# Third pair's first layer beside the first two's, attention vectors as columns, bias reliefs by rows, and a new table of priorities

## The chip, the cores and the metric

One core of a Trainium2 chip runs the whole program in one launch. The metric is the device time of one execution in microseconds. TensorE (PE) does matmuls, with its weight loads shown apart (PEld). VectorE (DVE), ScalarE (ACT) and GpSimd (POOL) do elementwise work. SyncE (SP) issues most of the DMAs, and ScalarE's queue issues a few at the start.

## The reference

64 graphs of 256 nodes with 256 features go through two layers, in float32. All that matters here:

```python
# layer 0
def _gat(h, adj, W, a, out_features):
    Wh = h @ W
    e = leaky_relu(Wh @ a[:256] + swap(Wh @ a[256:]), 0.2)
    att = softmax(where(adj > 0, e, NEG), axis=1)
    return att @ Wh
h = _gat(_gat(x, adj, W1, a1), adj, W2, a2)
h = layernorm(x + h, g_ln1, b_ln1)
x = layernorm(h + relu(h @ w_ff1 + b_ff1) @ w_ff2 + b_ff2, g_ln2, b_ln2)
# layer 1, 8 heads of 32
attn = softmax(q @ k.T / sqrt(32))
out = sum over r in 0..3 of (attn * (adj == r)) @ v_r      # adj is 0 or 1 here
x = layernorm(x + out @ Wo + bo, g1, beta1)
x = layernorm(x + gelu(x @ W1 + b1) @ W2 + b2, g2, beta2)
```

## The kernel before

**Pairs.** The kernel works on pairs of graphs, 32 of them. Each pair is a Python generator, `whole_way` (line 1212), that goes through two GAT layers (`gat_layers`, 637), a feed-forward with ReLU (`feed_forward`, 813), the relational attention (`attention`, 955), and a second feed-forward with GELU. Several pairs are on their way at once. Large products are done by a 2x2 block scheme with seven products in place of eight (`Blocks`, 470; `by_seven`, 887). Every matmul of 128 output columns is issued as four strips of 32 (`by_strips`, 161), each in two instructions.

**The order is planned in Python, when the program is built.** `run` (286) simulates the engines with a clock for each. The generators yield steps of TensorE, each with the events it needs, a number of PSUM banks and the buffers it takes. Pieces for the other engines are queued with `put` (221), with an estimated duration. At each turn the engine that can begin first begins. Among several pairs with a step ready, TensorE takes the one of lowest `degree` (294), and another engine takes the piece of lowest `rank`. At most `flight` pairs are on their way. `CHANGES` (32) alters ranks, degrees, `slack`, `flight` and the order of the block products ("first", "qkv") at given planned times. `START`, `LANDED` and `THERE` (67 to 69) are times the planner assumes for the first loads. The order that comes out is fixed: each engine runs its instructions in it.

**The start.** W1·W2 with the attention vectors beside it is made on the chip as `w12`, 260 columns (168 to 189): DVE multiplies W2's rows with a broadcast a2 and sums them (line 179), TensorE multiplies by W1's transpose, and DVE and ScalarE copy. The two a1 columns are loaded on ScalarE's queue (176). Meanwhile SP issues the loads of all weights, with those of the first three pairs (`EARLY`) between them (1142 to 1165).

**GAT layers.** For each graph pair: the product with `w12` (`ps<-w,...`, 260 columns), copies out of PSUM by ScalarE (642), exponentials of the attention columns (`addends`, 558, into a tile `rise`), then their rows spread over all partitions into a tile `rows`. For the first two pairs (`HURRIED`) this is done by TensorE (587) with ScalarE copies (590). For the others DVE turns the tile (597), and SP stores it to memory (601) and loads it back spread (605). `gat_weights` (612) forms the weights `e` on DVE (lines 622 and 624) and scales the values on ScalarE (631), and TensorE multiplies (`ps<-xw,e` or `ps<-v,e`). The values lie in two buffers `xw`, and those of pair 1 in the attention's buffer `v`. A pair from the third on waits until the pair before has begun its second layer's product and the pair before that is through its GAT layers:

```python
yield [loads[0], *([z_begun[pair - 1], through_gat[pair - 2]] if pair > 1 else [])], None, 2, *(["xw"] * (pair != 1))
```

**Reliefs.** Layer norm's scale and shift are handled so that a stage's output bias is added to the residual in advance. What this adds to the next stage's input must be taken out of that stage's bias: `relieve` (1172) computes bias minus W^T times the added vector, one column of output per matmul (line 1179, 128x128 weights and a moving operand of one column). It runs for the first feed-forward, q and k, and the second feed-forward. After each, DVE forms sums of weight blocks for the block scheme (438, 432).

**The end.** In the last stage `by_seven` leaves sums of rows to ScalarE (`means`, 705, line 712), then squares (726), the root on POOL (731, 732), two DVE passes (737, 740) and the store to `out` (1222), each for two tiles of rows at a time: graph 0, then graph 1.

Of the kernel before, what the change touches and what calls it, by code (L numbers as in the profile page):

```python
# [10 lines left out]
F32 = mybir.dt.float32  # L11
# [19 lines left out]
NORMED = ()  # L31
CHANGES = (
    (27.0, ("rank", "centre", 2),
     ("all", "first", ("a1", "b1", "a2", "a6", "b2", "b6", "a5", "a7", "b7", "b5", "a4", "b4", "a3"))),
    (117.0, ("rank", "piece", 3), ("rank", "halves", -1)),
    (207.0, ("all", "slack", 0.4), ("rank", "exp", -2), ("rank", "scale", 2)),
    (297.0, ("degree", "gat", -1)),
    (387.0, ("degree", "first", -1)),
    (477.0, ("rank", "halves", 2), ("rank", "v", -0.5)),
    (567.0, ("all", "slack", 0.1)),  # L40
    (657.0, ("all", "first", ("a1", "b1", "b2", "a2", "a6", "b6", "a5", "a7", "b7", "b5", "a4", "b4", "a3"))),
    (747.0, ("all", "slack", 0.6), ("rank", "act", -1), ("rank", "turn", 0), ("rank", "divide", 0), ("degree", "fill", 1.5),
     ("rank", "qk", 2)),
    (837.0, ("rank", "mask", -0.5), ("rank", "centre", 2)),
    (927.0, ("rank", "addends", 2)),
    (1017.0, ("rank", "means", -2), ("rank", "sums", -2), ("all", "slack", 0.4)),
    (1197.0, ("rank", "mask", 1)),
    (2187.0, ("rank", "mask", -0.5)),
    (2277.0, ("rank", "exp", -0.5), ("rank", "halves", -0.5)),
    (2457.0, ("rank", "squares", 3)),  # L50
    (2547.0, ("all", "slack", 0.3)),
    (2637.0, ("rank", "normalise", 1.5), ("degree", "first", 2)),
    (2727.0, ("rank", "centre", 1), ("rank", "turn", 1), ("all", "slack", 0)),
    (2817.0, ("all", "slack", 0.2), ("rank", "means", 3)),
# [6 lines left out]
        "normalise": -1, "copies": -2, "seeds": -2, "act": -1, "last": -1, "sums": -0.5, "qk": 1, "v": 1.5, "exp": 3, "mask": 0, "halves": 0, "invert": 3,  # L61
# [5 lines left out]
START = {"tensor": 9.5, "vector": 9.3, "scalar": 9.7, "gpsimd": 0.0, "sync": 36.0}  # L67
LANDED = (("ln0", 15.0), ("ff0", 18.5), ("ff0_last", 26.0), ("ln1", 28.5), ("attention", 34.5), ("ff1", 40.0), ("ff1_last", 43.0))
THERE = ((6.5, 8.0, 13.5), (9.5, 11.0, 27.5), (20.5, 22.0, 35.0))
# [3 lines left out]
def two_layers(ctx: ExitStack, tc: tile.TileContext, t: dict, out: bass.AP, flag: bass.AP):  # L73
# [22 lines left out]
    PART = 64  # L96
# [74 lines left out]
    a2, w1T = passing[:, 0], passing[:, 1].rearrange("p (c m) -> p c m", c=KC)  # L171
    junk = work.tile([P, 2, N], F32, name="h", bufs=HQ)[:, 0]
    nc.sync.dma_start(right[:, :, :D], t["L0_gnn_W2"].rearrange("(c p) m -> p c m", p=P))
    nc.scalar.dma_start(w1T, t["L0_gnn_W1T"].rearrange("(c p) m -> p c m", p=P))
    nc.scalar.dma_start(a2, bass.AP(tensor=t["L0_gnn_a2"].tensor, offset=t["L0_gnn_a2"].offset, ap=[[0, P], [1, 2 * D]]))
    nc.scalar.dma_start(right[:, :, D + 2:], t["L0_gnn_a1c"])
    for s in range(2):
        for c in range(KC):
            nc.vector.scalar_tensor_tensor(
                junk, right[:, c, :D], 1.0, a2[:, s * D:(s + 1) * D], op0=ALU.mult, op1=ALU.mult,  # L180
                accum_out=right[:, c, D + s:D + s + 1])
    both = [bank() for _ in range(KC)]
    for m in range(KC):
        for columns in (slice(0, D), slice(D, D + 4)):
            for c in range(KC):
                by_strips(both[m][:, columns], lhsT=w1T[:, c, m * P:(m + 1) * P], rhs=right[:, c, columns],
                          start=c == 0 and columns.start == 0, stop=c == KC - 1, skip_group_check=True)
    nc.vector.tensor_copy(w12[:, 0], both[0][:, :D + 4])
    nc.scalar.activation(w12[:, 1], both[1][:, :D + 4], AF.Copy)

# [7 lines left out]
               for at, *each in CHANGES for of, name, value in each]  # L202
# [3 lines left out]
                                             ("input", 1), ("rows", 1), ("e", 2), ("adj", 4), ("sums_yT", 1), ("sums_yTa", 1), ("x", 4))}  # L206
# [151 lines left out]
    def done_with(name):  # L358
        del alone[name]

# [197 lines left out]
    def addends(y, there, at, layer, pair):  # L558
# [9 lines left out]
        def largest():  # L568
            nc.vector.tensor_reduce(steep[:, pair, layer:layer + 1], y[:, :, at:at + 2], axis=AX.XY, op=ALU.max,
                                    apply_absolute_value=True)  # L570

        def exps():
            e1 = y[:, :, at].rearrange("p (b j) -> p b j", b=2)
            nc.scalar.activation(of_kind[:, 0::2], e1, AF.Exp, bias=shift[:, 0:1])
            nc.scalar.activation(of_kind[:, 1::2], e1, AF.Exp, bias=shift[:, 0:1], scale=ALPHA)
            nc.scalar.activation(ratio, y[:, :, at + 1], AF.Exp, scale=ALPHA - 1.0)

        put("vector", 0.15, largest, *there, rank=3)
        there = put("scalar", 0.6, exps, *there, rank=rank_of["exps"], function="exp")
        if pair < HURRIED:  # L580
            yield [there], None, 4, "rows"
            at_home["rows"] = rows = work.tile([P, 8, 4, 32], F32, name="rows")
            copied = []
            for n in range(4):
                p = bank()
                for j in range(2):
                    nc.tensor.transpose(p[:, j * P:(j + 1) * P], rise[:, j, 8 * n:8 * n + 1].to_broadcast([P, P]), ident)

                def copy(n=n, p=p):
                    nc.scalar.activation(rows[:, :, n], p[:, :N].rearrange("p (q c) -> p q c", q=8), AF.Copy)  # L590

                copied.append(put("scalar", 0.33, copy, took(0.3), rank=0, frees=["bank"]))
            return at_home, ratio, copied
# [14 lines left out]
        there = put("vector", 0.2, turn, there, rank=rank_of["addends"])  # L608
# [3 lines left out]
    def gat_weights(y, at, at_home, ratio, there, to, b):  # L612
# [3 lines left out]
        def weigh(j):  # L616
            k = 2 * b + j
            if j == 0:
                of["e"] = work.tile([P, 2, N], F32, name="e", bufs=2)
# [13 lines left out]
        there = put("vector", 0.93, lambda: weigh(0), *there, rank=rank_of["weigh"] + b / 2, needs="e")  # L633
        there = put("vector", 1.13, lambda: weigh(1), there, rank=rank_of["weigh"] + b / 2, frees=["rows"] * b)
        return of, put_each("scalar", 0.4, [lambda j=j: scale(j) for j in range(2)], there, rank=rank_of["ratios"])

    def gat_layers(pair, to, loads):
        yield [loads[0], *([z_begun[pair - 1], through_gat[pair - 2]] if pair > 1 else [])], None, 2, *(["xw"] * (pair != 1))
        y = in_values if pair == 1 else work.tile([P, 4, D + 4], F32, name="xw", bufs=2)

        def evacuated(to, k, wide, ps):
            return put("scalar", 0.27, lambda: nc.scalar.activation(to[:, k, :wide], ps[:, :wide], AF.Copy),
                       took(0.88), rank=rank_of["evac"], frees=["bank"])

# [11 lines left out]
        at_home, ratio, there = yield from addends(y, there, D + 2, 0, pair)  # L656
        e = [gat_weights(y, D + 2, at_home, ratio, [loads[1], *there], to, b) for b in range(2)]
        there = []
        for b in range(2):
            yield [e[b][1]], None, 2, *(["xw"] if b == 0 else [])  # L660
            if b == 0:
                happens(z_begun[pair], clock["tensor"])
                z = work.tile([P, 4, D + 4], F32, name="xw", bufs=2)
            for i in range(2):
# [4 lines left out]
                there.append(evacuated(z, 2 * b + i, D + 2, ps))  # L669
            frees_at(clock["tensor"], ["e"])  # L670
        frees_at(clock["tensor"] + 0.2, ["xw"] * (pair != 1))
        at_home, ratio, there = yield from addends(z, there, D, 1, pair)
        e = [gat_weights(z, D, at_home, ratio, there, to, b) for b in range(2)]
        normal = {}
        for b in range(2):
# [7 lines left out]
            frees_at(there.time, ["e"] + ["xw"] * b)  # L683
            added = add_rows(to["x"], ps, b, there, loads[2])
            transposed(to["x"], layernorm(to["x"], ln[0], b, added, biased[0], stage="gat"), normal, b, pair, 0)
# [19 lines left out]
    def means(y, b, *events):  # L705
# [3 lines left out]
        def mean(j):  # L709
            if j == 0:  # L710
                of["less"] = small.tile([P, 2], F32, name="less", bufs=8)
            nc.scalar.activation(unread, y[:, 2 * b + j, :], AF.Copy, scale=-1.0 / D, accum_out=of["less"][:, j:j + 1])
# [3 lines left out]
    def layernorm(r, gb, b, added, *events, stage=None):  # L716
# [3 lines left out]
        rows = [r[:, 2 * b + j, :] for j in range(2)]  # L720
# [7 lines left out]
        def root():  # L728
# [4 lines left out]
            if stage in NORMED:  # L733
                nc.gpsimd.tensor_tensor(of["less"], of["less"], rstd, ALU.mult)
# [7 lines left out]
        def normalise(j):  # L742
            nc.scalar.activation(rows[j], rows[j], AF.Identity, bias=of["less"][:, j:j + 1], scale=rstd[:, j:j + 1])

        def onto_all(n, op):
            both = r[:, of_graph(b), :]
            nc.vector.tensor_tensor(both, both, gb[n].rearrange("p (k d) -> p k d", k=1).to_broadcast([P, 2, D]), op)

        there = put_each("scalar", 0.54, [lambda j=j: square(j) for j in range(2)], there, rank=rank_of["squares"])
        if stage in NORMED:  # L750
            there = put("gpsimd", 1.6, root, there, rank=0)
            there = put_each("scalar", 0.42, [lambda j=j: normalise(j) for j in range(2)], there, rank=rank_of["normalise"])
            return put_each("vector", 0.6, [lambda n=n, op=op: onto_all(n, op) for n, op in ((0, ALU.mult), (1, ALU.add))], there, *events,
                            rank=rank_of["scale"])
# [58 lines left out]
    def feed_forward(y, normal, w, func, relieved, gb, pair, stage):  # L813
# [44 lines left out]
        yield from (by_seven if stage in SEVEN else by_eight)(y, normal, f, evacuated, w2, w2_there, b, order)  # L858
# [829 lines left out]
```

## Time and profile before

| what | us |
|---|---|
| median of 3 runs | 2898.7 (2896.8 to 2900.65) |
| the profiled execution | 2905.58 |
| its span, first to last instruction | 2903.8 |
| TensorE busy in it | 2862.7 |
| mean granted TensorE clock | 0.996 of full |

The profile is one execution. "Busy" for TensorE is from the first to the last of its overlapping matmuls, so that a matmul which runs slowly counts as busy all the same; durations of equal groups must be compared to see this. In rows of the timeline the columns are start, duration, engine, line, operation, tiles, shape and count, with the idle time before it and what ended it in brackets. In rows of the chain they are start, duration, engine and tile. TensorE spends its time as follows (line, engine, operation, tiles, shape and count, then busy time, mean of one in ns, and idle time before):

```profile
L164 PE MATMUL ps<-w_L_gnn_W,ff 128*32 128x128 f32 x14336 | 424.4, 273 | 1.4 <-issue 0.8
L164 PE MATMUL ps<-w_L_gnn_w_ff,ff 128*32 128x128 f32 x14336 | 423.3, 273 | 1.9 <-DVE ff L509 1.1
L164 PE MATMUL ps<-yT,w_L_gnn_W1p 128*32 128x256 f32 x5120 | 307.6, 381 | 4.0 <-DMA yT<-home 2.6
```

These are the feed-forwards' second and first layers, the largest groups; each has a few us of idle time before it in the whole run.

### The profile page before, as it was taken

How to read it: one execution, taken by the hardware profiler on the slowest of the kernel's cores; microseconds unless marked ns; L12 is line 12 of the kernel's file. 1: busy time of each engine (PE TensorE's matmuls, PEld its weight loads, DVE VectorE, ACT ScalarE, POOL GpSimd, SP SyncE). 2: the span in 40 equal slices, each digit the busy share in tenths (PEclk: the TensorE clock that was granted, in tenths of full speed). 3: DMA queues.
4: the chain of work that ended last, by engine and by line, in shares of the span. 5: the costliest groups of instructions: out<-in, count | busy, mean ns of one | idle time of the engine just before them, and what ended most of it. 6: DMA issues, size and time to landing. Idle time of an engine off the chain costs nothing.

```text
span 2903.8 us, 151915 instructions
## 1 busy us (share of the span) xinstructions
PE 2862.7 (99%) x68114; PEld 2021.2 (70%) x68114; DVE 2636.2 (91%) x5873; ACT 1908.4 (66%) x5171; POOL 284.9 (10%) x518
## 2 busy tenths in 40 slices
PE   8999999999999999999999999999999999999997
PEld 5766677676776676676767776766777877767666
DVE  7889998899998999998999999999999999999986
ACT  5656766656766667666677666676666676666765
POOL 0001010101010100001111101101101111010001
PEclk9999999999999999999999999999999999999999
DMA  6222222222222221222222222222222222221100
GB/s 206 75 68 70 69 65 79 72 79 79 65 69 76 83 83 58 78 70 79 79 76 69 69 76 84 74 74 70 72 76 83 76 65 68 83 73 51 54 3 25
DMA packets 207955, 212.11 MB, mean 73 GB/s; under 512 B 22592, under 2 KB 166336, under 8 KB 207040
## 3 DMA queue, kind: packets, MB, share of 16 engines
q1 hardware_dynamic: 206608, 201.79, 21.6%
q8 instruction: 536, 8.78, 1.3%
q14 instruction: 123, 1.01, 0.1%
q10 hardware_dynamic: 688, 0.53, 0.1%
HBM read 137.51 MB, written 64.73 MB: 70 GB/s over the span
## 4 chain that ended last, share of the span: by engine, by line
PE 87%; DVE 6%; DMA 4%; ACT 1%; issue 1%; SPq 1%; ACTq 0%; DVEq 0%; POOL 0%; POOLq 0%
PE ps L164 73%; PE ps L1063 7%; PE ps L1031 4%; PE ps L1066 2%; DMA home<-yb 2%; DVE ff L913 1%; DVE m L1045 1%; DMA yT<-home 1%; SPq L784 1%; DMA rows<-row 1%; DVE x L740 1%; DVE yb L773 1%; DVE h L1049 0%; DVE x L737 0%; DVE x L910 0%
## 5 line engine op out<-in xcount | busy, mean ns | idle before, releaser
L164 PE MATMUL ps<-w_L_gnn_W,ff 128*32 128x128 f32 x14336 | 424.4, 273 | 1.4 <-issue 0.8
L164 PE MATMUL ps<-w_L_gnn_w_ff,ff 128*32 128x128 f32 x14336 | 423.3, 273 | 1.9 <-DVE ff L509 1.1
L164 PEld LDWEIGHTS ps<-w_L_gnn_W,ff 128*32 128x32 f32 x14336 | 393.3, 110 | 41.7 <-issue 19.5
L164 PEld LDWEIGHTS ps<-w_L_gnn_w_ff,ff 128*32 128x32 f32 x14336 | 396.2, 110 | 36.3 <-issue 10.0
L1041 ACT ACTIVATE a<-ps 128x512 f32<-128x512 f32 x512 | 264.3, 601 | 186.5 <-PE ps L1031 180.6
L913 DVE TENSOR_TENSOR ff<-ff 128x1024 f32<-128x1024 f32 x256 | 311.5, 1217 | 55.3 <-PE ps L164 38.9
L731 POOL TENSOR_SCALAR rstd<-squares 128x2 f32<-128x2 f32 x256 | 78.8, 308 | 2591.1 <-ACT unread L726 2590.6
L164 PE MATMUL ps<-yT,w_L_gnn_W1p 128*32 128x256 f32 x5120 | 307.6, 381 | 4.0 <-DMA yT<-home 2.6
L1045 DVE TENSOR_TENSOR m<-a,adj 128x1024 f32<-128x1024 f32 x256 | 307.9, 1215 | 3.7 <-ACT a L1041 3.5
L164 PE MATMUL ps<-yT,w_L_gnn_w_ff1p 128*32 128x256 f32 x5120 | 306.2, 379 | 0.0
L838 ACT ACTIVATE ff<-ps 128x512 f32<-128x512 f32 x384 | 220.9, 587 | 129.6 <-PE ps L164 128.9
L726 ACT ACTIVATE unread<-x,less 128x256 f32<-128x256 f32 x512 | 258.7, 505 | 70.6 <-DVE less L701 54.1
L509 DVE TENSOR_TENSOR ff<-ps,ff 128x512 f32<-128x512 f32 x384 | 255.6, 682 | 38.0 <-PE ps L164 25.2
L1000 ACT ACTIVATE qk<-ps,bqk 128x256 f32<-128x256 f32 x256 | 109.6, 470 | 222.6 <-PE ps L164 222.3
L164 PE MATMUL ps<-xw,e 128*32 128x256 f32 (+1 forms) x4032 | 245.0, 383 | 1.3 <-ACT xw L631 1.3
L164 PEld LDWEIGHTS ps<-yT,w_L_gnn_W1p 128*32 128x32 f32 x5120 | 165.3, 110 | 109.3 <-ACT ff L838 7.5
L164 PEld LDWEIGHTS ps<-yT,w_L_gnn_w_ff1p 128*32 128x32 f32 x5120 | 168.2, 110 | 99.9 <-ACT ff L838 0.5
L737 DVE SCALAR_TENSOR_TENSOR x<-x,less,b_ln 128x256 f32<-128x256 f32 x512 | 227.4, 477 | 7.3 <-ACT unread L726 6.2
L740 DVE SCALAR_TENSOR_TENSOR x<-x,rstd,b_ln 128x256 f32<-128x256 f32 x512 | 229.1, 477 | 1.3 <-POOL rstd L732 1.3
L910 DVE TENSOR_TENSOR x<-ps,x 128x256 f32<-128x256 f32 (+1 forms) x384 | 193.7, 505 | 21.9 <-PE ps L164 17.3
L732 POOL TENSOR_TENSOR rstd<-rstd,mhalf 128x2 f32<-128x2 f32 x256 | 205.5, 803 | 21.3
L164 PEld LDWEIGHTS ps<-xw,e 128*32 128x32 f32 x4032 | 135.7, 111 | 84.1 <-issue 2.6
(141 smaller groups left out, 4992.7 us busy)
## 6 DMA issues: line engine op xcount, KB each, us to landing
home<-yb SPq DMA_DIRECT2D x182, 256.0 KB, 2.2
yT<-home SPq DMA_DIRECT2D x728, 64.0 KB, 2.1
rows<-row SPq DMA_DIRECT2D x60, 512.0 KB, 4.0
x<-in_x SPq DMA_DIRECT2D x32, 512.0 KB, 3.9
out<-x SPq DMA_DIRECT2D x64, 256.0 KB, 2.5
input<-in_xT SPq DMA_DIRECT2D x30, 512.0 KB, 4.1
input<-in_adjT SPq DMA_DIRECT2D x29, 512.0 KB, 4.2
m<-in_adjT SPq DMA_DIRECT2D x3, 512.0 KB, 8.6
```

What stands on the lines that cost most here:

```text
L164: nc.tensor.matmul(to[at:at + DH], lhsT=lhsT[:, at:at + DH], rhs=rhs, **flags)
L509: nc.vector.tensor_tensor(self.target(*where), self.bank["z"], self.target(*where), ALU.add)
L726: nc.scalar.activation(unread, rows[j], AF.Square, bias=of["less"][:, j:j + 1], accum_out=squares[:, j:j + 1])
L732: nc.gpsimd.tensor_tensor(rstd, rstd, mhalf[:, :2], ALU.pow)
L737: nc.vector.scalar_tensor_tensor(rows[j], rows[j], of["less"][:, j:j + 1], g, op0=ALU.add, op1=ALU.mult)
L740: nc.vector.scalar_tensor_tensor(rows[j], rows[j], rstd[:, j:j + 1], beta, op0=ALU.mult, op1=ALU.add)
L838: return put("scalar", 0.5, lambda: nc.scalar.activation(target(c, h), of, AF.Copy), event, rank=rank_of["copies"])
L910: return put("vector", us, lambda: nc.vector.tensor_tensor(to, of, to, ALU.add), *events, rank=rank_of["last"], frees=frees)
L913: return put("vector", 1.14, lambda: nc.vector.tensor_tensor(to, a, b, op), *events, rank=rank_of["sums"])
L1041: nc.scalar.activation(a[n][q][:, k], ps[2 * q + k], AF.Exp)
L1045: nc.vector.tensor_tensor(m[n][q], a[n][q], adj, ALU.mult)
L1063: nc.tensor.matmul(po[o * DH:(o + 1) * DH, :N], lhsT=v[:, b, jc, at:at + DH], rhs=e[o // 2][:, o % 2, jc * N:(jc + 1) * N], start=r == jc ...
```

## The change

Six things are done at once.

1. **Weight setup.** W2's products with a2 are made by TensorE out of W2's transpose and a2's columns, in place of DVE. The four columns of a2 and a1 are one load on SP, second after W2. The wide product no longer waits for them.
2. **The third pair.** Its loads of x transposed and adj are issued right after those of the first two pairs. Its first layer no longer waits for the pairs before. For this, the first two pairs keep the values between their GAT layers in buffers of the attention's exponentials ("a"), with their two attention columns in small tiles of their own (`z_thin`). Pair 1 also has `rows` in a mask buffer ("m") and `e` in buffers of half sums ("h"). `rise` becomes a resource that the planner knows.
3. **Reliefs by rows.** The vector, spread over 32 columns, is the stationary operand, and the weights are the moving one; DVE turns the result into columns.
4. **The last stage of the last pair** is normalised and stored by row halves of both graphs in place of graph by graph.
5. **A new table `CHANGES`**, 25 entries for 20, with `flight` 5 from a planned time of 45.9 to 2673.9, and new assumed times of the first loads.
6. Code that nothing used (`NORMED`) is taken out.

```diff
 CHANGES = (
-    (27.0, ("rank", "centre", 2),
-     ("all", "first", ("a1", "b1", "a2", "a6", "b2", "b6", "a5", "a7", "b7", "b5", "a4", "b4", "a3"))),
-    (117.0, ("rank", "piece", 3), ("rank", "halves", -1)),
...
+    (9.9, ("rank", "rows", 1), ("rank", "exp", -2), ("rank", "ratios", 3), ("degree", "after", 0.5), ("degree", "first", 2.5),
+     ("all", "first", ("a1", "b1", "a6", "a2", "b2", "b6", "a5", "a7", "b7", "b5", "a4", "b4", "a3"))),
...
+    (2673.9, ("rank", "copies", 0), ("all", "flight", 7), ("degree", "attention", -1), ("rank", "qk", 0.5),
+     ("rank", "scale", 3), ("all", "slack", 0.1)),
...
-START = {"tensor": 9.5, "vector": 9.3, "scalar": 9.7, "gpsimd": 0.0, "sync": 36.0}
+START = {"tensor": 9.8, "vector": 9.7, "scalar": 9.7, "gpsimd": 0.0, "sync": 36.5}
...
-    nc.scalar.dma_start(a2, bass.AP(tensor=t["L0_gnn_a2"].tensor, offset=t["L0_gnn_a2"].offset, ap=[[0, P], [1, 2 * D]]))
-    nc.scalar.dma_start(right[:, :, D + 2:], t["L0_gnn_a1c"])
...
+    nc.sync.dma_start(right[:, :, D:], t["L0_gnn_ac"])
+    nc.scalar.dma_start(w2T, t["L0_gnn_W2T"].rearrange("(c p) m -> p c m", p=P))
...
+    wide(0)
+    nc.vector.tensor_copy(w12[:, 0, :D], both[0][:, :D])
+    wide(1)
+    nc.scalar.activation(w12[:, 1, :D], both[1][:, :D], AF.Copy)
+    narrow_columns(thin[0], w2T, slice(D, D + 2))
+    nc.vector.tensor_copy(right[:, :, D:D + 2], thin[0][:, :, :2])
+    narrow_columns(thin[1], w1T, slice(D, D + 4))
+    nc.vector.tensor_copy(w12[:, :, D:], thin[1])
...
-    for pair in range(2):
+    for pair in range(EARLY):
         emit[pair][0]()
         emit[pair][1]()
...
-    emit[2][0]()
-    emit[2][1]()
...
-        yield [loads[0], *([z_begun[pair - 1], through_gat[pair - 2]] if pair > 1 else [])], None, 2, *(["xw"] * (pair != 1))
+        yield [loads[0], *([z_begun[pair - 1], through_gat[pair - 2]] if pair >= EARLY else [])], None, 2, *(["xw"] * (pair != 1))
...
+        def in_parts(z, thin, k, ps):
+            def copy():
+                nc.scalar.activation(z[:, k, :D], ps[:, :D], AF.Copy)
+                nc.scalar.activation(thin[:, k], ps[:, D:D + 2], AF.Copy)
...
-                z = work.tile([P, 4, D + 4], F32, name="xw", bufs=2)
+                z = work.tile([P, 4, D + 4], F32, name="xw", bufs=2) if pair > 1 else rows_in("a")
+                thin = z[:, :, D:D + 2] if pair > 1 else z_thin[pair]
...
-    def relieve(bias, w, rows, more):
+    def relieve(bias, per, w, more):
 
         p = bank()
...
+        for h in range(2):
             for c in range(KC):
...
+                for q in range(HQ):
+                    nc.tensor.matmul(p[q * DH:(q + 1) * DH, h * per * DH:(h + 1) * per * DH],
+                                     lhsT=more[1][:, c:c + 1].to_broadcast([P, DH]),
+                                     rhs=w[:, ((0, 1), (2, 6))[h][c]].rearrange("p (a q j) -> p q a j", q=HQ, j=DH)[:, q],
+                                     start=c == 0, stop=c == KC - 1)
+        turned = p[:, 256:256 + 2 * per * DH]
+
+        def subtract():
+            nc.vector.transpose(turned, p[:, :2 * per * DH])
+            nc.vector.tensor_tensor(bias, bias, turned.rearrange("p (h a i) -> p h a i", h=2, i=DH)[:, :, :, 0], ALU.subtract)
...
-        normal["added"] = [means(y, g, d24, d7, d3) for g in range(2)]
+        if last_of_all(pair, stage):
+            normal["added"] = [means(y, by_halves(j), d24, d7, *([d3] * j)) for j in range(2)]
+        else:
+            normal["added"] = [means(y, pair_of(g), d24, d7, d3) for g in range(2)]
```

## The prediction

> **What bounds the kernel now.** I read the page's busy shares first, then the windows of the middle, then the chain of waits and the timeline of the start, then the end.
>
> ```profile
> PE 2862.7 (99%) x68114; PEld 2021.2 (70%) x68114; DVE 2636.2 (91%) x5873; ACT 1908.4 (66%) x5171; POOL 284.9 (10%) x518
> 1409.00:1497.00 88.00, 88.00 (x2120) 61.63 (x2112) 81.71 (x183) 59.35 (x161) 9.52 (x16) 1.00 0.24 75
> 1481.78 7.08 PE ps L164 x192
> 1569.82 7.08 PE ps L164 x192
> ```
>
> The second line is one window of the middle (length, then busy time of PE, PEld, DVE, ACT, POOL, granted clock, DMA share, GB/s): TensorE is busy in all 88.00 us, VectorE in 81.71. The last two are pieces of the chain of waits: the same piece comes back after 88.04 us, one pair of graphs. 32 pairs at 88.04 are 2817.3 us; the other 86.5 us of the span of 2903.8 are the start, the end and irregular stretches. TensorE's visible idle time is 2903.8 - 2862.7 = 41.1 us. I add the timeline's gaps: 4.56 before its first matmul, 3.8 + 2.1 + 1.3 up to 60 us, and 11.9 after its last matmul (2891.9). So 17.4 us lie scattered between.
>
> At the start the chain and the timeline show where time goes:
>
> ```profile
> 1.79 8.33 DMA xw<-in_L_gnn_a1c
> 22.27 3.47 PE ps L1179 x32
> 38.83 1.88 PE ps L1179 x16
> 42.57 3.66 PE ps L1179 x32
> ```
>
> The first is the load of the columns of a1: 2 KB, third on ScalarE's queue, landed at 10.1. The other three are the bias reliefs, 9.0 us of chain.
>
> ```profile
> 12.38 5.36 PE L164 MATMUL ps<-w,input 128*32 128x260 f32 x64
> 17.55 3.70 PE L164 MATMUL ps<-w,qk 128*32 128x260 f32 x64
> 27.11 4.80 PE L164 MATMUL ps<-xw,e 128*32 128x258 f32 x64
> 46.16 5.35 PE L164 MATMUL ps<-xw,e 128*32 128x256 f32 x64
> 25.00:30.00 5.00, 5.00 (x50) 3.21 (x52) 4.68 (x13) 3.30 (x9) 0.00 (x0) 0.66 0.81 276
> 45.00:50.00 5.00, 5.00 (x52) 3.18 (x55) 2.38 (x8) 1.35 (x3) 0.00 (x0) 0.66 0.39 111
> ```
>
> Sixty-four matmuls of nearly one size take 3.70, or 4.80 to 5.36. The two windows say why: a mean clock of 0.66 over 5 us. If it is half speed for a while, that is 2 x 0.34 x 5 = 3.4 us at half, 1.7 us lost, each time just after a long relief.
>
> **The change, part by part**, against the profiled execution (2905.6 us; span 2903.8).
>
> *Weight setup.* Now: the first product of pair 0 begins at 12.38, behind the a1 columns (10.1) and four DVE products (7.78 to 9.6, waiting for the broadcast a2). After: W2's transpose takes the place of the a2 broadcast, same 256 KB, same place in ScalarE's queue, so I land it at 7.78 like its predecessor. Wide parts: the first ran 4.56 to 6.50, the second, of the same size (1.7 when it ran at 10.5), ends near 8.2. Narrow parts: 16 narrow matmuls took 0.2 us, so 32 take 0.4, plus 0.2 until the copy starts and 0.2 for the copy (128x8: 0.16): 0.8 per round, two rounds, 9.8; with semaphores **10.0**. Gain 2.4. The open cost is the landing of the column load. By the nearest row (8.33 us for a 2 KB load of 8-byte pieces) it lands at 1.22 + 8.3 = 9.5, the product begins at 11.2 and the gain is 1.2. The Trainium skill ("DMA: Bandwidth & Descriptors", "Anatomy of one DMA") puts a fixed cost of about 2 us on a DMA besides its bytes (its fit is for the GpSimd path): landed by 4, and nothing lost. The a1 row was third behind 512 KB on its queue; the new load is second on SP, behind W2 alone, whose landing took 3.4 us. So I take 4.6 to 5, not the row. It also delays xT of pair 0 (landed 7.8) by one issue, 0.45: 8.3, still ahead of 10.0. The slow clock (the weight loads close up only at 15.8) could end sooner or stretch over more of an earlier product: -1.7 to +1, taken as 0.
>
> *Reliefs by rows.* Same number of matmuls (32) for a feed-forward bias, but 32 columns wide over 128 columns: the row of that size (feed-forward's second layer, x64 in 1.93 us) gives 0.9 us for 32. For the q/k bias 32 over 64 columns replace 16: 0.5. From 9.0 to 2.3: **-6.7**. Then the clock. The Trainium skill ("TensorE: Matmul & The Clock Gate", "The HAM clock gate") says that the clock is halved after about 3.4 us of *idle* time. By that rule a relief costs only its duration, since TensorE issues all through it. The windows say otherwise: low clock right after the reliefs of 3.47 and 3.66 us, none after the one of 1.88. By the row the two long ones cost 1.7 each on top: -3.4, and -10.1 in all; by the rule -6.7. I take the row as the ceiling. Each relief adds a DVE transpose (128x256: 0.45), together 1.15, ahead of its subtraction; what waits behind it on DVE are GAT weights.
>
> *Pair 2's first layer early; buffers in exp, masks, half sums.* Its product (3.70, now at 52.46) loses its waits for the earlier pairs and can run behind pair 1's. It covers the gaps that shorter reliefs would uncover (TensorE waits 2.08 for pair 1's scaled values at 33.99, 1.3 for pair 1's second layer at 59.2). Its loads (2 x 512 KB) pass x of pair 0 and the first feed-forward weights on SP: about 1 MB at 380 GB/s, 2.7 us later for those; x is first read at 49.6, and the weights' relief can wait behind the product. Its attention weights can't come as early: their row goes through SP, which issues first loads until 35.5, then 1.8 and 4.0 us to land (medians of issues): about 42, against 60.3 now. ScalarE gets 8 copies of two columns (0.2 each, from the ratio rows): 1.6, inside its 9 idle us between 22 and 46.
>
> *What DVE lets through.* Between 22 and 46 DVE is busy 22.02 of 24 us, between 46 and 70 20.83. So TensorE's possible gain at the start, 2.4 + 10.1 + 3.4 idle = 15.9, isn't all to be had: the weights' two passes (0.48 each, eight pairs of them a layer for two pairs of graphs) come next. DVE begins them at 22.34 and could begin 2.4 earlier; its idle time from there to 70 is 5.2, of which I give it 3.5; and block sums of later weights that it does at 41 to 66 (some 7 us) can move behind 70, where it was busy 15.2 of 18: 3 us. Sum 8.9. **Start: -9**, between -4 (DVE binds, nothing deferred) and -16.
>
> *Last stage.* Rows are taken by halves, so half of the squares no longer wait for the last product. ScalarE is what binds there: four means (0.6) and four squares (0.65) from 2891.26 to 2896.48, in whatever order; only its gap of 0.4 goes, and less work stands behind the last square: **-0.7** (-0.3 to -1.5). The outputs stay two of 256 KB.
>
> *New table of priorities.* It changes the order for all pairs and the profile of before shows none of it. In the regular stretch there is nothing to win. Of the 17.4 scattered idle us, with low clock after two of them (292 and 2835, 1.7 each), I take **-2.5**; ends -12 (most of it) and +14 (0.45 us a pair in some 30 pairs). One pair fewer in flight should be harmless: a pair's way takes about 3.9 periods (1504 to 1848), and there are four x buffers.
>
> Sum -9 - 0.7 - 2.5 = -12.2: 2891.6 span. The profiled run is 6.9 above the median of 2898.7; I keep that distance and take the sum from the median: **2886.5**.
>
> **Rivals.**
> - *DVE is the bound of the start* (0.2): only the earlier begin and little deferral count: -4, -0.7, nothing from the table: 2894. For it: 22.02 of 24 us. Against: its block sums are of lowest rank and can wait.
> - *All of TensorE's start is won* (0.17), reliefs, clock and gaps, and some scattered waits too: -16 - 0.7 - 6 = 2876. Against: DVE's share.
> - *Slower: a wait comes into every pair* (0.13). Place: a block product that waits for DVE's sum (L509), now six waits of at most 1.1 us in the whole run. Price: 0.6 us x 30 pairs = 18, against -9.7: 2907. It decides from 9.7 / 30 = 0.32 us a pair. For it: DVE has only 6.3 us to spare in 88, and the table reorders DVE's pieces in every stage. Against: the dependences between them are as before.
> - *The early product doesn't come early*: TensorE reaches it only where the order puts it; then reliefs and setup alone are left, near the first rival's 2894 (within its 0.2).
>
> **Numbers.** Forecast 0.5 (own range 2880 to 2891), the rivals 0.2, 0.17, 0.13. Within 0.2%, 5.8 us, is about what a measurement of this kernel can't tell from no change. Faster (below 2892.9): 0.5 + 0.17 + 0.08 of the first rival = 0.75. Same: 0.12 of it = 0.12. Slower: 0.13. Range 2873 to 2898: it leaves out most of the slower case and the far end of the fast one.
>
> **What would show it.** The a1 wait gone and the first 260-column product near 10.0; reliefs under 1 us each with a clock of 1.0 behind them; pair 2's product right behind pair 1's; the first feed-forward matmul (now 60.94) near 52; the period still 88.04. Wrong: a period above 88.3, DVE under 90% between 20 and 46 while TensorE idles, or new windows of low clock.

## The result, and the profile after

| | before | changed |
|---|---|---|
| median | 2900.01 us (16 runs) | 2892.88 us (16 runs) |
| lowest and highest | 2896.8 to 2901.82 | 2889.64 to 2896.41 |
| the profiled execution | 2905.58 | 2890.66 |
| its span | 2903.8 | 2888.8 |

The ratio is 0.9976, with a 95% interval from 0.9968 to 0.9984: 7.1 us faster. The two profiled executions lie on opposite sides of their medians (5.6 above, 2.2 below), so the traces differ by 15.0 us where the kernels differ by 7.1. What follows of the traces has to be read with that.

Where did the time come from? First, a view by stretches: the start and two parts of the middle. Columns are stretch, length, busy time of PE, PEld, DVE, ACT and POOL with instructions, granted clock, DMA share, GB/s. Before:

```profile
0.00:88.00 88.00, 76.32 (x1304) 50.81 (x1308) 63.87 (x193) 48.85 (x132) 4.55 (x14) 0.96 0.52 177
88.00:1232.00 1144.00, 1134.74 (x27103) 794.27 (x27095) 1052.12 (x2336) 755.84 (x2054) 109.32 (x204) 1.00 0.23 73
1232.00:2817.00 1585.00, 1580.22 (x37897) 1123.13 (x37893) 1457.66 (x3220) 1056.71 (x2855) 162.68 (x284) 1.00 0.22 70
```

The changed kernel:

```profile
0.00:88.00 88.00, 71.18 (x1312) 42.77 (x1316) 62.25 (x197) 50.36 (x143) 4.99 (x14) 0.90 0.55 188
88.00:1232.00 1144.00, 1136.83 (x27192) 802.24 (x27184) 1055.51 (x2348) 755.55 (x2062) 111.44 (x204) 1.00 0.23 72
1232.00:2817.00 1585.00, 1583.95 (x38088) 1124.43 (x38088) 1467.27 (x3212) 1084.27 (x2885) 151.14 (x285) 1.00 0.22 70
```

Read the counts of PE, not its busy time. By 88 us both kernels have issued nearly the same number of matmuls (1304 and 1312), and the changed kernel's count holds 48 more for its setup and reliefs (192 against 144), so it is 40 behind in the pairs' own work. **The start, for which most of the change was made, gains nothing in the trace**, and its mean clock has dropped from 0.96 to 0.90. In the next stretches the changed kernel does 89 and 191 more. At the stretch's own mean (1585 / 38088 = 0.042 us a matmul) the three differences are -1.7, 3.7 and 8.0 us; the other 5.0 of the 15.0 lie in the end.

The start was ahead for a while. Without setup and reliefs, the matmuls begun by 46 us are 288 before and 360 in the changed kernel, by 70 us 680 and 676. What the early steps won is lost between 46 and 70 us.

The first steps came as foreseen. TensorE's timeline of the changed kernel, lines that answer to those shown of before:

```profile
9.94 3.71 PE L174 MATMUL ps<-w,input 128*32 128x260 f32 x64 [0.30 <-DVE w L205]
13.47 7.20 PE L174 MATMUL ps<-w,qk 128*32 128x260 f32 x128
...
21.62 1.08 PE L1198 MATMUL ps<-w_L_gnn_w_ff1p,c_L_gnn_b_ff2c 128*32 128x128 f32 x32
...
26.00 4.07 PE L174 MATMUL ps<-xw,e 128*32 128x258 f32 x40 [2.28 <-ACT xw L653]
...
45.42 5.95 PE L174 MATMUL ps<-a,e 128*32 128x256 f32 x64 [4.64 <-ACT a L653]
...
57.73 1.93 PE L822 MATMUL ps<-ident,x 128*32 128x128 f32 x32 [2.22 <-DVE x L770]
60.38 1.93 PE L174 MATMUL ps<-yT,w_L_gnn_w_ff1p 128*32 128x256 f32 x16 [0.71 <-ACT yT L826]
```

The first product begins at 9.94 (before 12.38). The third pair's product stands right behind the second's. The reliefs take about 1 us. But waits of 2.28, 4.64 and 2.22 us have come in, and behind them matmuls run for some us at about half speed: 40 took 4.07 us and 64 took 5.95, where 64 took 3.71 at 9.94. The first feed-forward matmul, last line, begins at 60.38; before it was 60.94. Three windows around those places have a granted clock near one half:

```profile
26.00:30.00 4.00, 4.00 (x40) 1.82 (x40) 3.83 (x16) 1.62 (x7) 0.00 (x0) 0.57 0.90 222
43.00:50.00 7.00, 4.58 (x44) 2.18 (x48) 4.14 (x15) 3.67 (x9) 0.00 (x0) 0.52 0.50 148
57.00:64.00 7.00, 5.56 (x69) 3.10 (x72) 6.75 (x23) 2.68 (x6) 1.05 (x2) 0.52 0.01 2
```

Who made TensorE wait 4.64 us at 45.42? ScalarE's timeline of the changed kernel:

```profile
42.82 1.06 ACT L406 ACTIVATE adj<-input 128x1024 uint8<-128x1024 int32 x1 [2.91 <-DMA input<-in_adjT]
43.78 1.19 ACT L611 ACTIVATE m<-ps 128x256 f32<-128x256 f32 x4
44.84 0.92 ACT L653 ACTIVATE a<-a,rs 128x256 f32<-128x256 f32 x2
```

ScalarE runs its fixed order. Next is a copy of the *fourth* pair's adjacency into bytes, whose load has not landed; it stands 2.91 us, and the row copies and scaled values that TensorE wants queue behind it. Nothing in the wait's name (`ACT a`) tells of that load. In the kernel before the same copy waits too:

```profile
44.50 1.06 ACT L386 ACTIVATE adj<-input 128x1024 uint8<-128x1024 int32 x1 [2.21 <-DMA input<-in_adjT]
```

There TensorE did not wait: it was at its long third relief (42.57, 3.66 us), and its product followed without a gap at 46.16. The relief was cover.

### The profile page after: what moved, and what is told of

The parts are those of the page before. It is cut to its first block, busy times and chain, and to the rows that moved or that the text cites. A ratio compares the mean times of both kernels' runs of the same rounds, so it can differ in the third digit from the quotient of the medians.

```text
span 2888.8 us, 151957 instructions
## 1 busy us (share of the span) xinstructions
PE 2852.2 (99%) x68162; PEld 2014.9 (70%) x68162; DVE 2637.6 (91%) x5869; ACT 1928.2 (67%) x5201; POOL 275.9 (10%) x518
## 4 chain that ended last, share of the span: by engine, by line
PE 92%; DVE 3%; DMA 2%; ACT 1%; SPq 1%; issue 1%; POOL 0%; POOLq 0%; DVEq 0%; ACTq 0%
PE ps L174 78%; PE ps L1084 7%; PE ps L1052 4%; PE ps L1087 2%; DMA home<-yb 1%; DMA yT<-home 1%; SPq L802 1%; DVE x L770 0%; DVE x L928 0%; PE ps L822 0%; DVE x L767 0%; DVE ff L931 0%; DMA input<-in_adjT 0%; DVE yb L791 0%; DVE ff L529 0%
## 5 line engine op out<-in xcount | busy, mean ns | idle before, releaser
L763 POOL TENSOR_SCALAR rstd<-squares 128x2 f32<-128x2 f32 x256 | 72.0, 281 | 2585.5 <-ACT unread L758 2584.4
L174 PE MATMUL ps<-yT,w_L_gnn_w_ff1p 128*32 128x256 f32 x5120 | 316.3, 380 | 0.7 <-ACT yT L826 0.7
L174 PE MATMUL ps<-yT,w_L_gnn_W1p 128*32 128x256 f32 x5120 | 314.3, 379 | 1.8 <-ACT ff L856 1.0
L174 PE MATMUL ps<-xw,e 128*32 128x258 f32 (+1 forms) x3904 | 234.4, 383 | 2.7 <-ACT xw L653 2.7
L862 ACT ACTIVATE ff<-ff,c_L_gnn_b_ff 128x256 f32<-128x256 f32 x384 | 174.8, 502 | 79.2 <-DVE ff L529 79.1
L862 ACT ACTIVATE ff<-ff,c_L_gnn_b 128x256 f32<-128x256 f32 x384 | 174.5, 506 | 23.1 <-DVE ff L529 21.5
```

The lines of the kernel that those rows point to most:

```text
L174: nc.tensor.matmul(to[at:at + DH], lhsT=lhsT[:, at:at + DH], rhs=rhs, **flags)
L862: evacuated[h][m] = put("scalar", 0.4, lambda m=m, to=to, source=source: nc.scalar.activation(to, source, func, bias=b1[:, m:m + 1]), even ...
```

## The experiments

**Table and structure apart.** Theory A: the gain is the table's. Theory B: it is the structure's. *old_table* is the changed kernel with the table of before, *table_alone* the reverse; *gated* is the changed kernel in which the third pair waits for the first two again.

```diff
 CHANGES = (
-    (9.9, ("rank", "rows", 1), ("rank", "exp", -2), ("rank", "ratios", 3), ("degree", "after", 0.5), ("degree", "first", 2.5),
...
+    (27.0, ("rank", "centre", 2),
...
```

> The changed kernel with the table of priorities of before. Theory A (the gain comes from the order in the middle and at the end; what the start saved came back there as waits): most of the gain goes, 2898 to 2906 us, ratio to before 0.9995 to 1.002, with scattered TensorE waits after 88 us again. Theory B (the gain comes from the parts at the start: setup, reliefs, early product): the gain stays, 2890 to 2895, ratio 0.997 to 0.9985.

> The kernel before with the new table of priorities alone. Theory A: most of the gain is there, 2889 to 2895 us, ratio 0.9965 to 0.9985. Theory B: nothing of it, 2898 to 2906, ratio 0.9995 to 1.002.

```diff
-        yield [loads[0], *([z_begun[pair - 1], through_gat[pair - 2]] if pair >= EARLY else [])], None, 2, *(["xw"] * (pair != 1))
+        yield [loads[0], *([z_begun[pair - 1], through_gat[pair - 2]] if pair > 1 else [])], None, 2, *(["xw"] * (pair != 1))
```

> The changed kernel, where the third pair waits for the pairs before it as it did before. Theory A (TensorE waits for others in the start anyway): the product moves behind 45 us, more idle TensorE before, start about as long, time within 5 us of the changed kernel. Theory C: the order of everything later is another draw, 2890 to 3100, with a period of the pairs other than 88.

Measured: old_table 3165.38 us, ratio 1.0936 (1.0913 to 1.0959). table_alone 2990.59, 1.032 (1.0306 to 1.0334). gated 3068.81, 1.0587 (1.0572 to 1.0601). All are far slower than either kernel. Theories A and B both fall; for *gated*, so does the time within 5 us, and only the wide range of Theory C holds. The loss is hardly at the start: by 88 us old_table, table_alone and gated have issued 1172, 1248 and 1265 matmuls. In *old_table* it comes from waits that recur over the whole run. TensorE's waits in old_table (tile waited for, sum, times, longest):

```profile
PE ps L163 <- DVE qk L1096: 70.2, 23, 8.6
PE ps L163 <- DMA yT<-home: 50.1, 13, 9.6
```

A table is no term of its own in a sum. It fits the structure it was set with, and each swap costs 10 to 40 times what the change brings.

**Parts undone in an unchanged order.** So the next kernels keep every engine's order, and only the instructions differ. *old_reliefs* has the matmuls of one column again, *old_setup* the old weight setup, *by_graphs* the last stage graph by graph; *changed_again* repeats the changed kernel.

```diff
-                    nc.tensor.matmul(p[q * DH:(q + 1) * DH, h * per * DH:(h + 1) * per * DH],
...
+                    nc.tensor.matmul(p[:, h * per + a:h * per + a + 1], lhsT=w[:, ((0, 1), (2, 6))[h][c], a * P:(a + 1) * P],
+                                     rhs=more[1][:, c:c + 1], start=c == 0, stop=c == KC - 1)
```

> The changed kernel, same order on every engine, with the reliefs' matmuls of before (one output column each, no transpose on VectorE). Theory A, with the third relief as the cover of a wait of ScalarE for the fourth pair's adj (landed at 42.8 us): within 2 us of the changed kernel, 2891 to 2895 us (ratio 0.997 to 0.9985); TensorE's wait of 4.6 us before its product at 45.4 shrinks to about 2, and the first feed-forward matmul stays within 1 us of 60.4. Theory B (reliefs and clock are worth 6.7 to 10 us): 2899 to 2903, first feed-forward matmul at 66 or later.

```diff
-    narrow_columns(thin[0], w2T, slice(D, D + 2))
...
+    nc.scalar.dma_start(right[:, :, D + 2:], t["L0_gnn_a1c"])
...
```

> The changed kernel, same order on every engine, with the weight setup of before (first product near 12.4 us, not 9.9). Theory A (later waits are pinned by a load that lands at 42.8): 2891 to 2895 us, first feed-forward matmul still within 0.7 us of 60.4. Theory B: 2.4 us slower, 2895 to 2896.5, first feed-forward matmul near 62.8.

```diff
-        return (pair, stage) == (NPAIR - 1, 2)
+        return False
```

> The changed kernel, the last stage by graphs as before; only the end's order differs. By the traces (12.3 us from the last matmul to the end before, 10.5 after): 1.7 us slower than the changed kernel. By the prediction: 0.7.

> The changed kernel itself, as the partner of the other runs on the same chip: 2889 to 2893 us, ratio 0.9968 to 0.9984 if its gain over before doesn't depend on the chip. If the old reliefs and the old setup really cost time (ratios 0.9989 and 1.0002 in the runs before), this stays near 0.9976; if those differences were the chip's, it is near 0.999.

| | median us | ratio to before (95%) |
|---|---|---|
| changed_again | 2892.35 | 0.9973 (0.9963 to 0.9983) |
| old_reliefs | 2893.86 | 0.9989 (0.9983 to 0.9996) |
| old_setup | 2897.91 | 1.0002 (0.9994 to 1.001) |
| by_graphs | 2892.36 | 0.9977 (0.997 to 0.9985) |

The gain repeats. Against the changed kernel's 0.9976, undoing the reliefs costs 0.0013 (3.8 us of 2900), the setup 0.0026 (7.5 us), each give or take 3 us; the halves of the last stage nothing that can be measured. TensorE's timeline of old_reliefs shows cover at work:

```profile
41.98 3.73 PE L1198 MATMUL ps<-c_L_gnn_b2c,w_L_gnn_W1p 128*128 128x1 f32 x32
47.89 6.13 PE L174 MATMUL ps<-a,e 128*32 128x256 f32 x64 [0.87 <-ACT a L653]
```

The three reliefs are 6.5 us longer (3.63 + 1.95 + 3.73 against 1.08 + 0.63 + 1.06), but the product behind them begins at 47.89, only 2.5 us later than at 45.42: the wait before it has shrunk from 4.64 to 0.87. The first feed-forward matmul comes at 62.85, between the two theories, as the ratio does.

As the order is the same, one instruction's start can be compared across the traces. ScalarE's square (line 758) that the changed kernel begins at 91.35 begins at 91.30 in changed_again, 91.14 in by_graphs, 94.01 in old_reliefs and 91.16 in old_setup. So in these executions the undone reliefs still cost 2.7 us by then, and **the undone setup nothing**: its first product began at 11.97, 2.0 us late, but the wait of 4.64 us shrank to 3.59, and the granted clock from 22 to 46 us was 1.00 in place of 0.87, which may be this execution's luck. The 7.5 us of old_setup are therefore not what the setup takes at the start. Its trace falls behind later, first at a longer wait for VectorE with low clock behind it (0.66 from 130 to 135 us, 1.00 in the changed kernel). The changed kernel, then old_setup:

```profile
129.48 1.95 PE L174 MATMUL ps<-w_L_gnn_w_ff,ff 128*32 128x128 f32 x64 [1.64 <-DVE ff L931]
129.87 2.83 PE L174 MATMUL ps<-w_L_gnn_w_ff,ff 128*32 128x128 f32 x64 [2.23 <-DVE ff L931]
```

By 500 us it is 3.4 us behind, at the end 6.7, in many small steps. Why an equal order waits longer there stays open.

**The wait taken away.** If that load is what ate the start, the cure is to let ScalarE do the row copies first. In *adj3_later* the planner is told that the fourth pair's adjacency lands 4 us later; the load itself stays where it is.

```diff
-            return put("sync", 0.45, emit, *after, rank=3, lag=2.3, kb=512, **more)
+            return put("sync", 0.45, emit, *after, rank=3, lag=2.3 + more_lag, kb=512, **more)
...
-            adj = in_bytes(there(adjT, needs="input"))
+            adj = in_bytes(there(adjT, more_lag=4.0 * (pair == EARLY), needs="input"))
```

> The changed kernel, with the planner told that the fourth pair's adj lands 4 us later, so that ScalarE's conversion of it stands behind the first two pairs' row copies and scalings. Theory A (the start is pinned by that conversion in ScalarE's queue): TensorE's wait of 4.6 us at 45.4 goes, the first feed-forward matmul comes at 55 to 57, and 3 to 5 us are won, 2886 to 2890, if the rest keeps its quality. Theory C (every change of early planned times throws the order of all later pairs, and its outcome is a draw): the start improves as said, but the pairs' period changes and the time is anywhere from 2885 to 3100.

2948.8 us, ratio 1.018 (1.0166 to 1.0194): slower, far from Theory A and inside Theory C's wide range. The start did nearly what was expected: waits of 1.03 and 1.84 us stand in place of the 4.64, and the first feed-forward matmul comes at 59.01, behind a whole second-layer product. A pair's product that the changed kernel begins at 1232.19 begins here at 1220.53. Behind it the spacing breaks. TensorE's timeline, first halves of the products of two graphs:

```profile
1220.53 1.94 PE L174 MATMUL ps<-w,input 128*32 128x260 f32 x32
...
1328.32 1.94 PE L174 MATMUL ps<-w,input 128*32 128x260 f32 x32
```

107.8 us where the changed kernel has 1232.19 and 1320.18, 88.0. This gave Theory C a cause: an entry of the table takes effect when the *planned* clock passes its time, so it was set for one step; a plan that reaches that step a few us sooner or later hands the entry to another, and from there on has another order. Two kernels test it. *adj3_shifted* is adj3_later with every entry from 603.9 on put 4 us later, as much as the planned landing moved. *table_early* is the changed kernel with nothing altered but those entries, 2 us earlier.

```diff
-    (603.9, ("degree", "rows", 1),
+    (607.9, ("degree", "rows", 1),
...
-    (693.9, ("rank", "weigh", 3), ("rank", "v", 3),
+    (697.9, ("rank", "weigh", 3), ("rank", "v", 3),
...
```

> As adj3_later, and every table entry from planned time 603.9 on stands 4 us later. Theory C (the entries belong to the steps they were set at; adj3_later was slow because its plan reaches those steps some us later, so that the entries catch others): the spacing of pairs goes back to 88 us from the tenth pair on, and the start's saving is kept (4.5 us less lost in the first 88 us, some 8 us ahead of the changed kernel later in adj3_later): 2884 to 2889. Rival B (the later mask copy of the fourth pair is itself what disturbs the order of the later pairs): the entries' times matter little, 2930 to 2955 as adj3_later.

> The changed kernel, and every table entry from planned time 603.9 on stands 2 us earlier; nothing else. Theory C: the first 600 us are the same and the pairs behind are not: entries catch other steps, spacing of pairs irregular somewhere behind 600 us, 2930 to 2965 in all. Rival B (an entry is good or bad by what it says, a shift of 2 us in 2900 is nothing): 2889 to 2897, as the changed kernel.

adj3_shifted: **2886.02 us, ratio 0.9952** (0.9938 to 0.9966), 7 us faster than the changed kernel and the fastest of all. table_early: 2958.91, ratio 1.0196 (1.0182 to 1.021). Both are inside Theory C's numbers and far from the rival's. The traces show the order itself. Against the changed kernel, VectorE's order in table_early is the same up to 748 us and another from there on, so 2 us on the entries are enough. In adj3_shifted it differs only from 43 to 212 us. That the new order of table_early costs time shows first where the spacing breaks, at the same pair as in adj3_later:

```profile
1229.24 1.94 PE L174 MATMUL ps<-w,input 128*32 128x260 f32 x32
...
1334.50 1.94 PE L174 MATMUL ps<-w,input 128*32 128x260 f32 x32
```

In adj3_shifted it doesn't, and the lead is kept to the end. The changed kernel's products at 1232.19 and 2550.65 are here:

```profile
1224.30 1.94 PE L174 MATMUL ps<-w,input 128*32 128x260 f32 x32
...
2543.07 1.94 PE L174 MATMUL ps<-w,input 128*32 128x260 f32 x32
```

7.9 and 7.6 us earlier; the spans differ by 7.5. TensorE's timeline of adj3_shifted at the place of the old wait, then ScalarE's:

```profile
41.01 1.09 PE L608 MATMUL ps<-ident,rise 128*128 128x128 f32 x8
43.13 3.67 PE L174 MATMUL ps<-a,e 128*32 128x256 f32 x64 [1.04 <-ACT a L653]
```

```profile
41.48 1.21 ACT L611 ACTIVATE m<-ps 128x256 f32<-128x256 f32 x4 [0.24 <-PE ps L608]
42.55 0.92 ACT L653 ACTIVATE a<-a,rs 128x256 f32<-128x256 f32 x2
43.35 1.07 ACT L406 ACTIVATE adj<-input 128x1024 uint8<-128x1024 int32 x1
```

The adjacency's copy now comes third and waits for nothing. TensorE waits 1.04 in place of 4.64, and the 64 matmuls behind take 3.67 in place of 5.95 us. The first feed-forward matmul is at 58.75 (60.38 in the changed kernel), with a whole second-layer product (`xw,e`, 32 at 56.99) already done before it. The lead is made early: the pair's product that the changed kernel begins at 288.46 begins at 280.92, 7.5 us sooner. But the copy is not all that moved: 154 of ScalarE's and 268 of VectorE's instructions stand elsewhere in the order between 43 and 212 us. And the waits only shrank a little; the clock did more. Busy us of TensorE, its granted clock, and busy us of VectorE, by windows:

| us | before | changed | adj3_shifted |
|---|---|---|---|
| 22 to 46 | 21.92, 0.93, 22.02 | 16.65, 0.87, 20.82 | 19.57, 1.00, 21.31 |
| 46 to 60 | 12.73, 0.88, 11.01 | 10.40, 0.74, 11.12 | 8.18, 1.00, 13.62 |
| 60 to 70 | 10.00, 1.00, 9.82 | 9.62, 0.81, 8.23 | 10.00, 1.00, 9.64 |
| TensorE idle, sum | 3.4 | 11.3 | 10.3 |

With the copy moved, the next long wait of TensorE is 2.92 us at 49.72, and there VectorE is busy 13.62 of 14 us.

**The parts again, in the mended order.** If cover explains why the reliefs were worth so little, they must be worth more here.

> adj3_shifted with the matmuls of the old reliefs (32, 16 and 32 of one column), same order on every engine. Theory A (in the changed kernel the reliefs' gain was eaten by the wait for the fourth pair's adj that came behind; with that wait short, a long relief costs all that the prediction gave it, 6.7 us and 3.4 of low clock): 2894 to 2898, ratio to before 0.998 to 0.999. Rival B (other waits behind the reliefs cover them as well, so that undoing costs some 4 us, as old_reliefs against the changed kernel): 2888 to 2892, ratio 0.996 to 0.997.

> adj3_shifted with the old weight setup, planned order unchanged. Theory A (the setup is worth what the first product begins earlier, 2 us): 2887 to 2889, ratio 0.9958 to 0.9964. Rival B (its ends catch the later order as well, the 8 us that old_setup lost against the changed kernel): 2892 to 2896, ratio 0.9975 to 0.9985.

| | median us | ratio to before (95%) |
|---|---|---|
| shifted_old_reliefs | 2893.4 | 0.9973 (0.9963 to 0.9983) |
| shifted_old_setup | 2887.81 | 0.9959 (0.9946 to 0.9972) |

The reliefs: 0.0021, or 6.1 us, between the two theories' numbers, and with 5 us of uncertainty the times don't decide. The trace speaks for Theory A, for its own execution:

```profile
43.77 4.82 PE L1198 MATMUL ps<-c_L_gnn_b2c,w_L_gnn_W1p 128*128 128x1 f32 x32
51.27 6.19 PE L174 MATMUL ps<-a,e 128*32 128x256 f32 x64 [0.87 <-ACT a L653]
```

The product begins 8.1 us later than in adj3_shifted (43.13), against 2.5 in the covered order, and then runs at about half clock. ScalarE's square that adj3_shifted begins at 88.11 begins here at 99.26, 11.2 us later, where the prediction gave 10.1 for reliefs and clock. That execution took 2898.49, 5 us over the kernel's median, so its sizes are the upper end. The setup: 0.0007, or 2.0 us with the same uncertainty, as Theory A had it; the rival's numbers lie outside the ratio's interval. The same square begins at 91.10 there, 3.0 us later.

## Why the prediction was right, and where it wasn't

- **Setup** (-2.4): the first product at 9.94, foreseen for 10.0. The column load landed 4.5 us after its issue at 1.24, at 5.7: later than the 4.6 to 5 taken, far sooner than the 9.5 of the row, and nothing waited for it. In time, 2.0 us in the mended order; in the changed order its trace shows nothing left of it at 91 us.
- **Reliefs** (-6.7, and -3.4 of clock): they measured 2.77 us in all (foreseen 2.3), and no low clock follows them directly. But these -10.1 were a ceiling for TensorE, and what was given back has the next line.
- **What DVE lets through** (start -9): this step failed. The sum took VectorE for the next limit and put the earliest loss of cover on it. What the shorter reliefs uncovered came back as waits: TensorE's idle time from 22 to 70 us rose from 3.4 to 11.3 us. The largest, 4.64 us, was ScalarE's order, at the copy of the fourth pair's adjacency. The prediction counted ScalarE's idle us as room for more copies, and did not ask what ScalarE was idle *for*. The third pair's product was to cover the gaps, but it ends at 20.7, before the first relief, and covers none of them. Nor did the sum price low clock behind new waits (0.74 from 46 to 60 us). The start lost about 1.7 us (40 matmuls by 88 us), where a gain of 9 was foreseen. adj3_shifted shows that most of it was there: with that copy behind two others, and the steps up to 212 us that the planner then orders otherwise, 7 us come back. How much of them is the copy's alone was not tried. That 2886.02 lies next to the 2886.5 foreseen says little: it is another kernel, with other parts.
- **Last stage** (-0.7): from the start of the last matmul the span has 10.5 us in the changed kernel and 11.2 in by_graphs, one execution each. The difference is the 0.7 foreseen, but the times can't tell it. Before it was 12.1, so some of the shorter tail isn't the halves' doing.
- **Table** (-2.5, ends -12 and +14): as a single term this was the wrong form. Alone it costs 3.2%, and without it the structure costs 9.4%. And the term was too small: by the counts above some 12 us of the 15.0 between the traces lie from 88 to 2817 us, and the two waits that the prediction named (292 and 2835) are the largest single losses that can be seen in the trace of before:

```profile
291.72 4.48 PE L164 MATMUL ps<-yT,w_L_gnn_W1p 128*32 128x256 f32 x48 [2.58 <-DMA yT<-home]
2834.40 1.25 PE L1063 MATMUL ps<-a,v 128*32 128x256 f32 x16 [3.05 <-ACT a L1041]
```

They are 5.6 us of waiting, and with the 1.7 us of low clock that the prediction counted behind each about 9 us, the second of them in the end. In the changed kernel no wait behind 88 us is longer than 1.64. That the new table in its own structure took them away is likely, but it was not tried alone. How much of the difference is the 7.8 by which the two profiled executions stray from their medians can't be split.
- **The sum**: -12.2 foreseen, -7.1 measured (0.9968 to 0.9984: -9.3 to -4.6). Direction and the wide range held; 2892.88 lies above the forecast's own 2880 to 2891, and the make-up did not hold. A start that lost where 9 were foreseen and a rest that won far more than its 3.2 offset each other, so that the sum came near is in part luck.
- **Signs**: the first product near 10.0, the third pair's right behind the second's and the period of 88.0 came. The first feed-forward matmul near 52 did not (60.38), and two of the signs of being wrong did: VectorE busy 87% from 22 to 46 us while TensorE idled, and new windows of low clock.
- **Rivals**: the slower one, a wait in every pair, didn't come: TensorE is busy 1583.95 of 1585 us from 1232 on. The nearest to the truth by its number is the first (2894), but its cause, VectorE, is only half there. At the largest wait VectorE idles too while ScalarE holds the queue (busy 4.14 of 7 us from 43 to 50); around the two shorter ones it is busy 3.83 of 4 and 6.75 of 7. That one pair fewer in flight is harmless was not tried alone.

## To carry to other kernels

Before taking a long instruction off the path, list what each *other* engine waits for during it, the loads of later work included: an engine with a fixed order that stands before a late load holds everything behind it, and the wait list names only the last link. Where an order is planned from a table keyed to planned times, no part can be judged by swapping parts of the source: undo it with the order held fixed, and when the plan moves by a few us, move the table's later entries with it. Compare traces by how many instructions of the same work are done at a given time, and set each trace against its kernel's median first. Where two kernels have the same order, subtract the start times of the same instruction: this shows where a difference arises, and old_setup's was not where its change was.

## What the runs showed of the hardware

The prediction took low clock to follow long reliefs. It also follows short waits, but not every one. In the changed kernel a wait of 2.28 us at 26.00 was followed by half clock (0.57 from 26 to 30); in adj3_shifted a wait of the same length was not:

```profile
27.72 1.95 PE L174 MATMUL ps<-xw,e 128*32 128x258 f32 x32 [2.28 <-ACT xw L653]
```

32 in 1.95 us is full speed. The same wait of 2.28 or 2.29 us stands in eight traces: in five, 40 matmuls behind it took 3.88 to 4.07 us (changed, changed_again, by_graphs, table_early, shifted_old_setup), in three, 32 took 1.95 (adj3_shifted, adj3_later, old_setup). The Trainium skill ("TensorE: Matmul & The Clock Gate", "The HAM clock gate") speaks of about 3.4 us of idle time; here low clock followed 2.28 us in five traces of eight, so length alone doesn't decide, and what does was not tried.

The start isn't alike either: the first product of adj3_shifted, the same 64 matmuls as in the changed kernel, begun at 9.81, took 5.57 us in place of 3.71. The granted clock reads 1.00 in both from 10 to 14 us, so this column does not show every slow stretch. The same holds for the first of the prediction's slow rows, 5.36 us at 12.38, where the granted clock reads 1.00 from 12 to 16 us: its windows of 0.66 explain only the two others. Such differences of 2 us an execution come on top of any change as small as these.
